# Sampling stream 1.7 images behind the gated stream instead of two, both streams made continuous, and the preparation of the next image moved to steps 89 to 186

## Chip, core and metric

The kernel runs on one core of a Trainium2 chip. The metric is device time in microseconds (us) of one execution; the time before is 12707.76 us, the median of three runs (12704.01 to 12716.35). All engines of the core work from their own in-order instruction streams: PE (TensorE, matmul), DVE (VectorE), ACT (ScalarE), POOL (GpSimd) and SP (SyncE, which here only starts transfers).

## What is computed

The input is 32 images of 128 channels by 32 by 32 pixels. Two layers follow each other, both with a residual:

```python
x = x + L0(_gn(x))      # group norm, encode 128->1024, causal 64-tap convolution per feature, gelu,
                        # gated linear unit 1024->2048, layer norm, decode 1024->128
x = x + L1(_gn(x))      # group norm, depthwise 3x3 conv gives offsets, 8x8 taps sampled bilinearly
                        # at (pixel + tap + offset), weighted per channel, batch norm, gelu
```

Layer 1 shares its offsets over all channels of a tap, so the kernel writes bilinear sampling as a matmul of image rows with hat functions max(0, 1 - |x - i|) times max(0, 1 - |y - j|).

## The kernel before

`ssm_convolution` (L186 on) does the group norm of layer 0, the encoding and the long convolution for all images, and leaves y in DRAM (`y_d`). `main_block` then does the rest in two streams that are woven together by hand; its instruction order is the order of the Python calls (`tc.manual_schedule()`), engine by engine.

**The gated stream** is `first_part(b)`, one image at a time: two halves of 512 pixels, eight feature blocks m each. A block is eight matmuls for the gate (`gpg`, L814), eight for the value (`gpv`, L837), one for the encoding (`gph`, L853) and one decode matmul (`gpo`, L742), all with 512 columns. ACT makes the sigmoid of the gate (`gs`, L821) and a square (`gq`, L874); DVE joins the terms (L845, L866); POOL sums for the layer norm (L738). Three PSUM buffers (`pglu`) rotate through gate, value and encoding. `close` (L764 on) ends a half: two matmuls with `davg` (`gpm`, `gpq`), of which ACT copies the first (`gm`, L765), and some ticks later a store of layer 0's result `x1_d` (L789).

**The sampling stream** is `second_part(b, steps)`: 17 packs of columns. For pack h, SP loads the x hats (`ds<-dhat`, L1116, two buffers) and the y hats (`dhy<-rel_d`, L1131, three half-pack buffers); ACT turns the y distances into hats (`hat_y`, L1151 and L1152); DVE multiplies both (`weights`, L1157); PE multiplies with the image windows (`dps`, L1233) into four PSUM buffers (`psam`); DVE scales by the tap weights (`prod`, L1249); POOL adds up (L1276, L1284). A pack counts as 12 steps, so an image has 204; a full pack has 16 slots, pack 8 has 8, the packs at the ends have 13 or 14.

**The preparation of the next image**, `prepare(b + 1)`, is a list of (step, action) that `second_part(b)` runs in its `due` calls: `fetch` x1 (SP), group norm (`total`, `mean`, `variance`, `normal` on ACT, PE and DVE), nine convolution taps (DVE), two `turn` (PE transposes, ACT copies), 16 `window` transfers, `largest`, `across`, `down` (DVE), two `lay` and four `spread` transfers that lay the distances out in DRAM (`rel_n`, `rel_d`), `gather` (`dr<-rel_d`, L1005), and eight `hat(k)`: ACT computes one of the eight x hats in two instructions (L1016, L1017) into the only buffer of its pool (`hatpool`, 1 buffer) and starts its store on ACT's own queue (`dhat<-dh`, L1018). So hat k waits until the store of hat k-1 has landed. `gather` reads only the x half of `rel_d`, which the first two spreads write. The transfers of SP and ACT take turns at eight completion semaphores, and each waits for the transfer that had its semaphore before, so that about eight are under way at most.

`run_along` (L578 on) weaves generators: it always advances the one whose done share of its total is smallest. Before, `first_part(0)` runs alone, `first_part(1)` runs with `opening()` (the preparation of image 0, then the first loads, given the total 90.0 and yielding 30 plus 51 steps of 1), then `first_part(b + 2)` runs with `second_part(b)`, each pair to its common end, and the last two images are sampled alone.

Of the kernel before, what the change touches and what calls it, by code (L numbers as in the profile page):

```python
# [16 lines left out]
B, C, H, W = 32, 128, 32, 32  # L17
# [559 lines left out]
def run_along(*streams):  # L577


    left = [[gen, float(total), 0.0] for gen, total in streams]  # L580
    while left:
        s = min(left, key=lambda e: e[2] / e[1])
        cost = next(s[0], None)
        if cost is None:
            left.remove(s)
        else:
            s[2] += cost


def main_block(nc, tc, const, ins, x, u_d, y_d, x1_d, out, offmax):  # L590
# [16 lines left out]
    T = 512  # L607
    YB = 11
    SB, HB = 2, 3
    KS = 16 * H  # L610
    ctx = ExitStack()
    with ctx:
# [78 lines left out]
        for i in range(2):  # L691
# [9 lines left out]
        prods = [  # L701
            one.tile([P, 8 * KS + H], F32, tag=f"prod{i}", name=f"prod{i}") for i in range(2)
        ]
# [3 lines left out]
        def at(t, offset, ap):  # L707
            return bass.AP(tensor=t.tensor, offset=t.offset + offset, ap=ap)
# [176 lines left out]
        FIRST = 2 * (KD * (2 * KD + 2) + 2) * MM  # L885
# [4 lines left out]
        def prepare(b):  # L890
# [37 lines left out]
            def taps(lo, hi):  # L928
                def run():
                    if lo == 0:  # L930
                        st["co"] = two.tile([P, L], F32, tag="img", name=f"dco_{b}")
                    co3 = st["co"].rearrange("p (h w) -> p h w", w=W)
                    v3 = st["v"].rearrange("p (h w) -> p h w", w=W)
                    for n in (4, 0, 1, 2, 3, 5, 6, 7, 8)[lo:hi]:
                        dy, dx = n // 3 - 1, n % 3 - 1
                        y0, y1 = max(0, -dy), H - max(0, dy)
                        x0, x1 = max(0, -dx), W - max(0, dx)
                        src = v3[:, y0 + dy : y1 + dy, x0 + dx : x1 + dx]
                        to = co3[:, y0:y1, x0:x1]
                        wn = off_w[:, n : n + 1]  # L940
                        if n == 4:
                            nc.vector.tensor_scalar(
                                to, src, wn, off_b, op0=ALU.mult, op1=ALU.add
                            )
                        else:
                            nc.vector.scalar_tensor_tensor(
                                to, src, wn, to, op0=ALU.mult, op1=ALU.add
                            )

                return run  # L950
# [25 lines left out]
            def lay(a):  # L976
                def run():
                    nc.sync.dma_start(
                        at(
                            rel_n[b % 2], a * ASTEP + LEAST + 7 * JSTEP,  # L980
                            [[KSTEP, 8], [-JSTEP, 8], [1, L]],
                        ),
                        st["rel"][a * 64 : a * 64 + 64].rearrange("p w h -> p (w h)"),
                    )

                return run

            def spread(a, side):
                def run():
                    nc.sync.dma_start(  # L990
                        at(
                            rel_d[b % 2], a * NCOL + side * SIDE,
                            [[NV, 64], [8 * CELLS, NU], [1, NV]],
                        ),
                        at(
                            rel_n[b % 2], a * ASTEP + LEAST - 7 * H + VBASE[side],
                            [[KSTEP - 1, 64], [H, NU], [1, NV]],
                        ),
                    )

                return run
# [7 lines left out]
            def hat(k):  # L1009


                def run():
                    if k == 0:
                        st["h"] = dram.tile([2, 8, SIDE], F32, tag="hat_d", name=f"dhat_{b}")
                    t = hatpool.tile([P, HSUB], F32, tag="hat", name=f"dh_{b}_{k}")
                    nc.scalar.activation(t, st["t"], AF.Abs, bias=minus[:, k : k + 1])  # L1016
                    nc.scalar.activation(t, t, AF.Relu, scale=-1.0, bias=const["one"])  # L1017
                    nc.scalar.dma_start(  # L1018
                        at(
                            st["h"], k * SIDE,  # L1020
                            [[HSUB, P // 2], [8 * SIDE, 2], [1, HSUB]],
                        ),
                        t,
                    )

                return run

            def turn(n):


                def run():
                    if n == 0:
                        st["vt"] = two.tile([P, NCHUNK, C], F32, tag="img", name=f"dvt_{b}")
                    ps = psam.tile([P, 4, C], F32, tag="sam", name=f"dtr_{b}_{n}")
                    for i in range(4):
                        lo = (4 * n + i) * P
                        nc.tensor.transpose(ps[:, i, :], st["v"][:, lo : lo + P], ident)
                    nc.scalar.copy(st["vt"][:, 4 * n : 4 * n + 4, :], ps)
                    if n == 1:
                        st["vt_d"] = dram.tile([L, C], F32, tag="vt_d", name=f"dvt_d_{b}")  # L1040
                        nc.scalar.dma_start(
                            st["vt_d"].rearrange("(n p) c -> p n c", p=P), st["vt"]
                        )
                        st["xw_d"] = dram.tile(
                            [2, W, 8, NWIN, C], F32, tag="xw_d", name=f"dxw_d_{b}"
                        )

                return run

            def window(side, r):  # L1050
                def run():
                    nc.sync.dma_start(
                        st["xw_d"][side, :, r],
                        at(
                            st["vt_d"], (12 * side + r) * W * C,
                            [[C, W], [2 * W * C, NWIN], [1, C]],
                        ),
                    )

                return run  # L1060

            def ready():
                images[b] = st["xw_d"], st["h"]

            steps = [
                (28, fetch), (35, total), (37, mean), (40, variance), (42, normal),
                *((44 + 3 * i, taps(i, i + 1)) for i in range(9)),
                (47, turn(0)), (50, turn(1)),
                *((54 + i, window(i // 8, i % 8)) for i in range(16)),
                (68, largest), (70, across), (74, down), (76, lay(0)), (77, lay(1)),  # L1070
                *((81 + 3 * i, spread(i // 2, i % 2)) for i in range(4)),
                (99, gather), *((109 + 9 * k, hat(k)) for k in range(8)),
                (178, ready),
            ]
            return steps

        NP = len(PACKS)
# [99 lines left out]
        def second_part(b, steps):  # L1177
# [6 lines left out]
            for n in range(NP):  # L1184
# [9 lines left out]
                for i in range(0, PIECES, 2):  # L1194
# [47 lines left out]
                    def scale(piece, side):  # L1242
                        for p, sd, frm, (ky, rows, v0, run, step, skew) in work:
                            if (p, sd) != (piece, side):
                                continue
                            wt = wk[:, table_of[n] : table_of[n] + m]
                            wt = wt[:, :, ky : ky + step * (rows - 1) + 1 : step]
                            at_y = prod[:, ky * KS + v0 - ky :]
                            nc.vector.tensor_mul(  # L1249
# [3 lines left out]
                                        at_y.ap[0], [H, m],  # L1253
                                        [step * (KS - 1) + skew, rows], [1, run],
                                    ],
# [15 lines left out]
                def row(ky, lo=0, hi=m):  # L1271
                    return prod[:, ky * KS + lo * H : ky * KS + hi * H]

# [30 lines left out]
        def measure(slots):  # L1304

            return slots * 8.0 + 40.0

        SECOND = 3 * PIECES * sum(measure(slots_of(n)) for n in range(NP))

        def opening():  # L1310

            yield 30.0
            for _, step in prepare(0):
                step()
                yield 1.0
            for i in range(SB):
                load_x(i)
            for i in range(HB):
                load_y(i)
            windows(0, 0)  # L1320
            for part in range(PARTS):
                hat_y(0, part)
                weights(0, part)
# [1 line left out]

        ctx.enter_context(tc.manual_schedule())
        run_along((first_part(0), FIRST))
        run_along((first_part(1), FIRST), (opening(), 90.0))
        for b in range(B):
            steps = prepare(b + 1) if b + 1 < B else []  # L1330
            if b + 2 < B:
                run_along(
                    (first_part(b + 2, last=(b + 2 == B - 1)), FIRST),
                    (second_part(b, steps), SECOND),
                )
            else:
                run_along((second_part(b, steps), SECOND))
        for _, step in ending:
            step()

# [144 lines left out]
```

## Time and profile before

| | |
|---|---|
| Median of three runs | 12707.76 us |
| The profiled execution | 12713.35 us, of which the span from first to last instruction is 12711.4 us |
| PE busy | 12198.8 us (96%) |
| POOL busy | 8975.3 us (71%) |
| DVE busy | 7803.7 us (61%) |
| ACT busy | 5485.8 us (43%) |
| Sampling, all `dps` matmuls | 23936 matmul instructions, 2753.9 us |
| Gate and value, `gpg` and `gpv` | 16384 matmul instructions, 7499.4 us |
| DMA | 2350.46 MB, 185 GB/s on the mean |
| Granted TensorE clock, mean | 0.973 |

Every float32 matmul shows as two matmul instructions. Busy times come from the profiled execution; a view by stages says more than these shares, because the kernel has stretches with and without each stream. In the stages the granted clock is given as a share of full speed, and DMA share is the mean busy share of the 16 DMA engines.

### The profile page before, as it was taken

How to read it: one execution, taken by the hardware profiler on the slowest of the kernel's cores; microseconds unless marked ns; L12 is line 12 of the kernel's file. 1: busy time of each engine (PE TensorE's matmuls, PEld its weight loads, DVE VectorE, ACT ScalarE, POOL GpSimd, SP SyncE). 2: the span in 40 equal slices, each digit the busy share in tenths (PEclk: the TensorE clock that was granted, in tenths of full speed). 3: DMA queues.
4: the chain of work that ended last, by engine and by line, in shares of the span. 5: the costliest groups of instructions: out<-in, count | busy, mean ns of one | idle time of the engine just before them, and what ended most of it. 6: DMA issues, size and time to landing. Idle time of an engine off the chain costs nothing.

```text
span 12711.4 us, 162031 instructions
## 1 busy us (share of the span) xinstructions
PE 12198.8 (96%) x51362; PEld 6670.1 (52%) x51362; DVE 7803.7 (61%) x14315; ACT 5485.8 (43%) x7823; POOL 8975.3 (71%) x11691
## 2 busy tenths in 40 slices
PE   7999899999999999999999999999999999999965
PEld 7999444444444444444444444444444444444444
DVE  5555126666666666666666666666666666666666
ACT  4344124444444444444444444444444444444443
POOL 2455127777777777777777777777777777777779
PEclk9999999999999999999999999999999999999976
DMA  7899236666766666667666676666666667667666
GB/s 237 266 277 277 74 82 181 180 183 186 188 179 179 177 177 188 181 177 186 179 185 180 185 188 180 178 176 177 188 180 182 184 179 186 181 181 188 180 183 182
DMA packets 1521951, 2350.46 MB, mean 185 GB/s; under 512 B 619586, under 2 KB 835266, under 8 KB 1520066
## 3 DMA queue, kind: packets, MB, share of 16 engines
q1 hardware_dynamic: 1382210, 2027.97, 60.4%
q10 hardware_dynamic: 89728, 177.76, 3.8%
q0 software_dynamic: 49152, 134.28, 3.5%
q8 instruction: 413, 6.77, 0.2%
q14 instruction: 448, 3.67, 0.1%
HBM read 2016.61 MB, written 407.02 MB: 191 GB/s over the span
## 4 chain that ended last, share of the span: by engine, by line
PE 81%; DMA 6%; POOL 5%; DVE 3%; SPq 2%; issue 2%; ACT 1%; ACTq 0%; DVEq 0%; POOLq 0%
PE gpv L837 25%; PE gpg L814 24%; PE dps L1233 16%; PE psy L320 5%; PE gph L853 3%; PE psz L237 3%; DMA ds<-dhat 3%; PE gpo L742 3%; POOL prod L1276 3%; POOL do L1295 1%; DMA dhy<-rel_d 1%; POOL gs L738 1%; SPq L1131 1%; DVE ds L1157 1%; DVE prod L1249 1%
## 5 line engine op out<-in xcount | busy, mean ns | idle before, releaser
L1276 POOL TENSOR_TENSOR prod<-prod 128x256 f32<-128x256 f32 (+3 forms) x7616 | 5797.4, 801 | 1112.8 <-DVE prod L1249 1112.8
L1249 DVE TENSOR_TENSOR prod<-dps,k_weight_slots 128x512 f32<-128x512 f32 (+16 forms) x8704 | 3124.2, 407 | 1615.3 <-PE dps L1233 1204.5
L814 PE MATMUL gpg<-gy,g_w_glu 128*128 128x512 f32 x8192 | 3759.6, 602 | 41.0 <-ACT gs L821 26.9
L837 PE MATMUL gpv<-gy,g_w_glu 128*128 128x512 f32 x8192 | 3739.8, 599 | 0.0
L1233 PE MATMUL dps<-ds,dxw 64*128 64x128 f32 (+14 forms) x23936 | 2753.9, 374 | 262.5 <-DVE prod L1249 229.6
L1157 DVE TENSOR_TENSOR ds<-ds,dhy 128x640 f32<-128x640 f32 (+2 forms) x2176 | 2363.9, 1127 | 784.5 <-ACT dhy L1152 426.9
L1233 PEld LDWEIGHTS dps<-ds,dxw 64*128 64x128 f32 x23936 | 1968.0, 196 | 1343.1 <-issue 432.0
L814 PEld LDWEIGHTS gpg<-gy,g_w_glu 128*128 128x128 f32 x8192 | 1519.9, 191 | 1963.2 <-issue 1907.1
L837 PEld LDWEIGHTS gpv<-gy,g_w_glu 128*128 128x128 f32 x8192 | 1509.7, 190 | 1878.6 <-issue 1878.6
L738 POOL TENSOR_TENSOR gs<-gs,gq 128x256 f32<-128x256 f32 x896 | 751.5, 859 | 1856.7 <-ACT gq L874 1856.7
L1151 ACT ACTIVATE dhy<-dhy,k_minus_y 128x640 f32<-128x640 f32 (+2 forms) x2176 | 1698.5, 781 | 483.4 <-DMA dhy<-rel_d 174.0
L1152 ACT ACTIVATE dhy<-dhy,one 128x640 f32<-128x640 f32 (+2 forms) x2176 | 1726.5, 793 | 71.1
L874 ACT ACTIVATE gq<-gr 128x512 f32<-128x512 f32 x448 | 281.3, 628 | 2557.7 <-DVE gr L866 2551.8
L845 DVE SCALAR_TENSOR_TENSOR gs<-gpv,k_b_glu,gs 128x512 f32<-128x512 f32 x512 | 383.9, 750 | 1357.8 <-PE gpv L837 1289.4
L821 ACT ACTIVATE gs<-gpg,k_b_glu 128x512 f32<-128x512 f32 x512 | 351.3, 686 | 1860.7 <-PE gpg L814 1846.8
L357 POOL DMA_DIRECT2D y_d<-yo x1024 | 590.0, 583 | 693.5 <-ACT yo L344 633.5
L1284 POOL TENSOR_TENSOR dacc<-dacc,prod 128x256 f32<-128x256 f32 (+6 forms) x1184 | 886.7, 749 | 55.2
L738 POOL TENSOR_TENSOR gs<-gs,gr 128x256 f32<-128x256 f32 x896 | 810.7, 925 | 0.0
L320 PE MATMUL psy<-toe,z 128*128 128x192 f32 x4096 | 668.0, 326 | 7.4 <-DVE z L242 5.5
L320 PEld LDWEIGHTS psy<-toe,z 128*128 128x128 f32 x4096 | 663.0, 196 | 11.7 <-DVE z L242 6.8
L335 DVE TENSOR_TENSOR psy<-psy,t 128x256 f32<-128x256 f32 (+2 forms) x768 | 333.7, 434 | 346.1 <-ACT t L328 329.3
L853 PE MATMUL gph<-gu,k_W_enc 128*128 128x512 f32 x1024 | 530.2, 600 | 0.4 <-DVE gs L845 0.4
(164 smaller groups left out, 6055.0 us busy)
## 6 DMA issues: line engine op xcount, KB each, us to landing
dhy<-rel_d SPq DMA_DIRECT2D x3264, 160.0 KB
ds<-dhat SPq DMA_DIRECT2D x832, 400.0 KB
ds<-dhat SPq DMA_DIRECT2D x448, 480.0 KB
dxw<-dxw_d SPq DMA_DIRECT2D x832, 224.0 KB
y_d<-yo POOLq DMA_DIRECT2D x1024, 128.0 KB, 4.2
gy<-y_d SPq DMA_DIRECT2D x512, 256.0 KB
u<-u_d SPq DMA_DIRECT2D x224, 512.0 KB
dhat<-dh ACTq DMA_DIRECT2D x256, 390.0 KB
```

What stands on the lines that cost most here:

```text
L320: nc.tensor.matmul(ps[:, c // 2, c % 2, :], rows[i][:, (g * CG + c0 + c) // 2, c % 2, :], toe[:, c0 + c, :], start=True, stop=True,)
L738: nc.gpsimd.tensor_add(to[:, cut], to[:, cut], more[:, cut])
L814: nc.tensor.matmul(gate, w_glu[:, k, D + m * P : D + m * P + P], ys[k], start=(k == 0), stop=(k == KD - 1),)
L837: nc.tensor.matmul(val, w_glu[:, k, m * P : m * P + P], ys[k], start=(k == 0), stop=(k == KD - 1),)
L853: nc.tensor.matmul(h, w_enc[:, m * P : (m + 1) * P], u, start=True, stop=True)
L1151: nc.scalar.activation(t, t, AF.Abs, bias=minus_y)
L1152: nc.scalar.activation(t, t, AF.Relu, scale=-1.0, bias=const["one"])
L1157: nc.vector.tensor_mul(s_of[h][:, cut], s_of[h][:, cut], t)
L1233: nc.tensor.matmul(to[side][:, :, :, r0:r1], xw[half, w, :], frm, start=True, stop=True,)
L1249: nc.vector.tensor_mul(bass.AP(tensor=at_y.tensor, offset=at_y.offset, ap=[at_y.ap[0], [H, m], [step * (KS - 1) + skew, rows], [1, run],], ...
L1276: nc.gpsimd.tensor_add(row(to, lo, hi), row(to, lo, hi), row(frm, lo, hi))
L1284: nc.gpsimd.tensor_add(to, to, total[:, slot * H : (slot + nj) * H].rearrange("p (s y) -> p s y", y=H),)
```

## The change

The streams become two generators, woven once: all gated images from 1 on, and `opening()` followed by all sampled images. Each image counts 1 in its stream, and `opening()` counts AHEAD = 0.7 in place of a whole image. The preparation steps get new numbers, and are sorted: the distance between hats is 4 steps in place of 9, and `gather` stands at 150, ahead of the last of the spreads (151). In `opening()` the steps are now in sorted order too.

```diff
+    AHEAD = 0.7
...
-                (28, fetch), (35, total), (37, mean), (40, variance), (42, normal),
-                *((44 + 3 * i, taps(i, i + 1)) for i in range(9)),
-                (47, turn(0)), (50, turn(1)),
-                *((54 + i, window(i // 8, i % 8)) for i in range(16)),
-                (68, largest), (70, across), (74, down), (76, lay(0)), (77, lay(1)),
-                *((81 + 3 * i, spread(i // 2, i % 2)) for i in range(4)),
-                (99, gather), *((109 + 9 * k, hat(k)) for k in range(8)),
-                (178, ready),
+                (89, fetch), (94, total), (96, mean), (99, variance), (101, normal),
+                *((103 + 3 * i, taps(i, i + 1)) for i in range(9)),
+                (106, turn(0)), (109, turn(1)),
+                *((113 + i, window(i // 8, i % 8)) for i in range(16)),
+                (129, largest), (131, across), (135, down), (137, lay(0)), (138, lay(1)),
+                *((142 + 3 * i, spread(i // 2, i % 2)) for i in range(4)),
+                (150, gather), *((154 + 4 * k, hat(k)) for k in range(8)),
+                (186, ready),
             ]
+            steps.sort(key=lambda e: e[0])
...
-        run_along((first_part(1), FIRST), (opening(), 90.0))
-        for b in range(B):
-            steps = prepare(b + 1) if b + 1 < B else []
-            if b + 2 < B:
-                run_along(
-                    (first_part(b + 2, last=(b + 2 == B - 1)), FIRST),
-                    (second_part(b, steps), SECOND),
-                )
-            else:
-                run_along((second_part(b, steps), SECOND))
+
+        def first_parts():
+
+            for b in range(1, B):
+                for cost in first_part(b, last=(b == B - 1)):
+                    yield cost / FIRST
+
+        def second_parts():
+
+            for cost in opening():
+                yield AHEAD * cost / 82.0
+            for b in range(B):
+                steps = prepare(b + 1) if b + 1 < B else []
+                for cost in second_part(b, steps):
+                    yield cost / SECOND
+
+        run_along((first_parts(), 1.0), (second_parts(), 1.0))
```

## Prediction

> **What bounds the kernel now.** I read the stages first, because the kernel has stretches with one stream and with both. The columns are stage, length, busy time of PE, PE's weight load, DVE, ACT and POOL, granted clock, DMA share and GB/s.
>
> ```profile
> core 0: us, PE busy (x) PEld busy (x) DVE busy (x) ACT busy (x) POOL busy (x), PEclk, DMA share, GB/s
> 1313.80:1572.70 258.90, 254.84 (x578) 111.39 (x579) 29.25 (x39) 26.22 (x37) 36.00 (x52) 0.97 0.11 39
> 1572.70:1854.90 282.20, 255.35 (x598) 113.10 (x597) 57.51 (x67) 57.29 (x76) 45.82 (x56) 0.95 0.26 68
> 1854.90:2195.40 340.50, 339.53 (x1347) 167.43 (x1345) 216.16 (x404) 151.64 (x204) 242.36 (x314) 1.00 0.66 177
> 12179.00:12449.20 270.20, 143.71 (x761) 111.17 (x760) 186.94 (x360) 130.48 (x170) 217.31 (x272) 0.61 0.77 202
> 12449.20:12680.20 231.00, 137.95 (x747) 109.50 (x748) 170.06 (x338) 97.58 (x126) 213.19 (x270) 0.63 0.72 197
> 12680.20:12711.40 31.20, 0.92 (x4) 0.15 (x3) 3.41 (x10) 1.15 (x1) 19.87 (x28) 0.50 0.06 20
> ```
>
> The rows are: gated image 0 alone; gated image 1 with the opening; one of 30 woven images; image 30 sampled alone, with the preparation of 31; image 31 alone; the rest. The 30 woven images take 12179.0 - 1854.9 = 10324.1 us, 344.1 each, with PE always at work: they are bound by PE. The last two images, 501.2 us, leave PE half idle. A gated image costs 258.9 us alone, so sampling costs 344.1 - 258.9 = 85 us when woven in and 231 us when alone. That difference is what a shorter lag can win. PE's waits in the woven stretch come next:
>
> ```profile
> PE gpm L764 <- POOL gs L738: 61.4, 30, 2.4
> PE dps L1233 <- DVE prod L1249: 43.7, 40, 3.8
> ```
>
> About 2.0 us an image at `gpm`, which the change leaves alone, and 1.5 us at `dps`. So there is next to nothing to win inside a woven image, and whatever newly stops PE is paid 30 times. Where the 1.5 us arises shows in 12 us windows of image 10:
>
> ```profile
> 5422.00:5434.00 12.00, 12.00 (x40) 5.62 (x39) 9.31 (x11) 2.88 (x5) 11.92 (x15) 1.00 0.41 139
> 5434.00:5446.00 12.00, 12.00 (x51) 5.92 (x50) 4.79 (x15) 3.67 (x8) 11.92 (x18) 1.00 0.97 128
> 5458.00:5470.00 12.00, 12.00 (x65) 6.60 (x65) 4.33 (x15) 3.84 (x5) 7.02 (x11) 1.00 1.04 277
> 5470.00:5482.00 12.00, 8.37 (x35) 5.48 (x34) 7.31 (x19) 3.55 (x4) 5.66 (x14) 0.72 0.92 228
> ```
>
> The spreads (issued from 5432 to 5448) fill the DMA engines (0.97, then 1.04); `ds` for the next pack comes late, DVE waits for it, PE loses 3.6 us. `gather`, behind gate inputs and `ds` in the same queue, makes ACT wait 11.56 us before hat 0, which costs nothing there, because ACT runs that far ahead of its place.
>
> **The change, part by part.** The program order of the changed kernel puts the start of gated image b + 2 into pack 5 of sampled image b: the lag is 1.69 images (81/82 of 0.7 for the opening). No computing instruction is added or removed, and POOL and its queue get nothing new to wait for.
>
> *Start.* Gated image 1 now runs 0.69 alone and 0.31 woven: 0.69 x 258.9 + 0.31 x 344.1 = 285.3 instead of 258.9: +26 us.
>
> *Opening.* Its stall is 282.2 - 258.9 = 23.3 us, and looks so:
>
> ```profile
> 1810.85 0.94 ACT L1016 ACTIVATE dh<-dr,k_minus 128x780 f32<-128x780 f32 x1 [1.50 <-DMA dhat<-dh]
> 1828.93 0.69 ACT L1151 ACTIVATE dhy<-dhy,k_minus_y 128x480 f32<-128x480 f32 x1 [16.16 <-DMA dhy<-rel_d]
> 1835.77 0.67 ACT L821 ACTIVATE gs<-gpg,k_b_glu 128x512 f32<-128x512 f32 x1
> 1836.49 9.97 PE L814 MATMUL gpg<-gy,g_w_glu 128*128 128x512 f32 x16 [25.28 <-ACT gs L821]
> ```
>
> ACT is held by the hat stores and the first y hats, the sigmoid queues behind, PE stands. Hats there start every 4.67 us (1806.19 to 1810.85), the opening's step was 258.9/90 = 2.88 us and becomes 0.7 x 258.9/82 = 2.21 us. The hats fall behind by 8 x 0.67 = 5 us more; the 26 us of gated work that followed the opening no longer covers the loads of pack 1, some 5 to 9 us. Bounds 0 and 25; I take +14 us.
>
> *Tail.* The first 5.2 packs of image 30 are now woven. By image 31's pack times (12.2, 18.3, 15.0, 14.5, 14.4, then 0.23 of 14.4, from the `dps` starts), they save 78 us; the preparation, 39 us (270.2 - 231.0), stays in the tail whole, since it begins at step 89. It is squeezed: 32 steps for eight hats are 32 x 1.13 = 36 us at 231/204 us a step, and a hat that had to wait took 7.45 us in this stage:
>
> ```profile
> 12367.83 0.93 ACT L1016 ACTIVATE dh<-dr,k_minus 128x780 f32<-128x780 f32 x1
> 12375.28 0.94 ACT L1016 ACTIVATE dh<-dr,k_minus 128x780 f32<-128x780 f32 x1 [3.19 <-DMA dhat<-dh]
> ```
>
> Eight are 60 us, 24 more than the steps give; bounds 0 and 25, I take +17. Tail: -61 us.
>
> *Woven images.* Fetch, group norm, taps, turns and windows keep their distances, and 0.69 of an image later they meet the gated stream where they met it before; the work, DVE and ACT under 65% busy, hides as before. Variance to normal falls into the short pack 8 (13 us instead of 20.7): ACT's 1.15 us square and 1.28 us table load then stand closer before a PE matmul, 0 to 1 us, I take 0.5. Spreads now fall in packs 11 and 12, followed by full packs, where before pack 8, half as big, gave relief. But `gather` now waits on SP for spread 1, ahead of the five gate loads; `dhy`, the last spread and `ds` of pack 14 queue behind it, and DVE and PE wait for those. Before, three spread issues held SP for 10.4 us anyway, so I see 0 to 4 us more of SP and, since `ds` now precedes the gate loads, about as much back. I let the old 1.6 us (1.5 as above and a trifle at `gpg`) go.
>
> What is new is the hats. Behind hat k on ACT stand `hat_y` of the next packs (DVE and then `dps` wait for them), the sigmoid and the copy `gm`; PE's next gate reuses `gpm`'s buffer and needs `gm` at once: in image 10, `gpm` ran at 5492.3, `gm` at 5493.3, the gate at 5494.9. In the changed order hat 5 stands just ahead of `gm`, with 6.5 us of PE work between (`dps` 2.2, four to five matmuls of 0.86), of which hat and copy need 2.6: ACT may be 4 us late. From hat 0 to hat 5 there are 20 steps of 20.7/12 us = 34.5 us. Five hats of 7.45 us need 37.3; hat 0 itself waits some 2.5 us for `gather` (three spreads ahead of it, 4 steps instead of 10). Late by 37.3 + 2.5 - 34.5 - 4 = 1.3 us. But the 7.45 us was in a stage of DMA share 0.77. The trace's packet records put the end of a hat store 2.3 us after its issue when the engines are idle (all of image 0), 7 to 8 us for hats 0 and 1 of nearly all later images, where the share is 0.9 to 1.0, and 3 to 4.5 us where it is below 0.6. In the new window the demand is: three packs at 11.5 us of all engines, spreads 13, gather 1.4, hats 6.4, gate inputs 4.2, about 60 of 65 us, where the old one measured 0.84. With two stores of 7.7, one of 5.6 and two of 4.4 us, each plus 2.35 us of ACT work and signalling, five hats take 41.6 us: late by 5.6 us. Between 1.3 and 5.6 I take 3.5.
>
> The Trainium skill's page "DMA: Bandwidth & Descriptors" (section "Anatomy of one DMA — SWDGE (gpsimd) path", so for GpSimd's transfers) prices one at a fixed 2.0 us plus bytes over 436 GB/s: 399 KB would land after 2.9 us, a hat would take 4.9 us, inside the 6.9 us of four steps, no wait at all; the woven image would gain 1.6. The opening's 4.67 us agrees with that, the woven images' 7 to 8 us don't. The same page (section "Issuing engines are not separate DMA queues") says why ACT's own queue is no way round: all issuers share 16 engines. I go by the rows of the loaded stretch.
>
> Sum an image: +3.5 + 0.5 - 1.6 = +2.4 us; 30 x 2.4 = +72. Total: 26 + 14 - 61 + 72 = +51 us on 12713.35, that is 12764; the runs' median lies 5.6 us lower, so 12759 us.
>
> **Rivals.** *The hats keep step* (on the other side): if a hat takes at most 7.2 us, (34.5 + 4 - 2.5)/5, ACT is never late and the spread's stall goes. Then the image gains 1.6, 48 us in all, and with the start and tail (-21) the time is 12708 - 69, about 12640. For it: the 4.67 and 7.45 us rows. Against it: the stores of 7 to 8 us. Chance 0.28.
>
> *A wash:* what the hats cost, the spread gives back; only start and tail remain, 12687 us. Chance 0.17.
>
> *Saturation throughout:* a hat takes 9 us to hat 5, late by 45 + 2.5 - 38.5 = 9 us, 7.9 net, 237 - 21 = +216: 12924 us. For it: spreads followed by full packs, `ds` late too. Against it: a stopped PE lets the DMA engines catch up. Chance 0.16. The likeliest case, 12733 to 12830, has 0.39.
>
> That the change does not do what it says is ruled out by the program order.
>
> **Range and chances.** About 0.2% (25 us) is what a measurement of this kernel can tell from no change. Faster 0.28, within 0.17, slower 0.55. From 12625 (a third of the first rival is below) to 12910 (half of the last is above): the cost of a woven image from -2 to +7.5 us.
>
> **What would show it.** A PE wait at `gpg` for ACT (`gm`) or at `dps` for DVE in packs 14 and 15 of every image, with ACT's `dh` waiting for `dhat<-dh` some 5 times an image (9 in all before): right. Woven images under 343 us: the first rival. Opening stall near 37 us and a tail of 470 us after the last gate confirm start and tail. If PE's new wait is for `gy` or `ds`, I priced the queue wrongly.

## The result, and the profile after

The changed kernel takes 12572.62 us (median of four runs, 12565.29 to 12590.62), beside 12709.51 us for the kernel before on the same chip: a ratio of 0.9893, 95% interval 0.988 to 0.9907. It is faster by 1.1%, where 0.4% slower was forecast. The profiled execution was the slowest of the four, 12590.62 us, its span 12588.9 us; so the profiles differ by 122.5 us and the medians by 136.9.

These are stages with the same columns as in the prediction. The first row is the kernel before, over its woven images from gated image 2 to 30. The others are the changed kernel: the same 29 images, one of them, the last woven image (31), image 30 alone, image 31 alone, the rest.

```profile
1854.90:11828.90 9974.00, 9870.93 (x38977) 4879.78 (x38976) 6403.01 (x11687) 4467.69 (x5972) 7571.55 (x9638) 0.99 0.68 181
1898.70:11777.20 9878.50, 9802.21 (x38978) 4834.91 (x38977) 6270.75 (x11688) 4522.82 (x6003) 7410.23 (x9658) 1.00 0.68 183
4968.40:5310.60 342.20, 337.90 (x1345) 166.47 (x1344) 215.48 (x404) 156.12 (x207) 254.94 (x334) 1.00 0.68 182
11777.20:12122.00 344.80, 339.45 (x1347) 167.02 (x1345) 217.18 (x411) 156.63 (x208) 258.30 (x337) 1.00 0.66 177
12122.00:12326.60 204.60, 105.05 (x516) 76.94 (x516) 132.56 (x248) 93.31 (x124) 140.52 (x175) 0.59 0.74 190
12326.60:12556.80 230.20, 138.29 (x747) 108.01 (x748) 169.51 (x338) 98.19 (x126) 214.65 (x271) 0.63 0.73 199
12556.80:12588.90 32.10, 0.85 (x4) 0.11 (x2) 3.36 (x10) 1.15 (x1) 19.83 (x28) 0.50 0.05 19
```

The time moved as follows. The last woven image ends in this table with its last gated matmul, at 12179.0 us before and 12126.5 us after; the rows above cut it 4.5 us sooner, at 12122.0.

| stretch, us | before | after | difference | predicted |
|---|---|---|---|---|
| start, to gated image 2 | 1854.9 | 1898.7 | +43.8 | +40 |
| 29 woven images, gated 2 to 30 | 9974.0 | 9878.5 | -95.5 | with the 30th: |
| woven image with gated 31 | 350.1 | 349.3 | -0.8 | +72 |
| after the last gate | 532.4 | 462.4 | -70.0 | -61 |
| span | 12711.4 | 12588.9 | -122.5 | +51 |

Start and end came within 9 us of the forecast. Nearly the whole error lies inside the woven images: 343.93 us each before, 340.64 after. Over the 29 images PE is busy for 9870.93 us before and 9802.21 us after, with the same matmuls. So PE not only waits less, its matmuls themselves take 68.7 us less. PE's waits in the woven stretch after are (total us, times, longest):

```profile
PE dtr L1038 <- DVE prod L1251: 34.1, 29, 1.2
PE gph L854 <- DVE gs L846: 26.2, 24, 3.1
PE dps L1235 <- DVE prod L1251: 12.0, 17, 1.1
PE gpm L765 <- POOL gs L739: 2.5, 3, 1.0
```

The wait at `gpm`, which the prediction left alone, is gone (61.4 us, 30 times, before), and so is most of that at `dps`. Two new ones, at `dtr` and `gph`, come once an image each but are short: of all waits over half a microsecond in these images, eight are longer than 1.3 us.

**Why `gpm` waits no more.** In the kernel before, this is POOL's timeline at the end of an image (start, duration, operation, count, idle time before):

```profile
5294.42 10.52 POOL L1276 TENSOR_TENSOR prod<-prod 128x224 f32<-128x224 f32 x14
5304.91 1.91 POOL L1284 TENSOR_TENSOR dacc<-dacc,prod 128x160 f32<-128x160 f32 x4
5306.92 4.69 POOL L1295 TENSOR_SCALAR do<-dacc,k_bn_mean,k_bn_var 128x1024 f32<-128x1024 f32 x1
5311.67 0.95 POOL L1183 MEMSET dacc<- 128x1024 f32 x1
5312.59 2.39 POOL L738 TENSOR_TENSOR gs<-gs,gr 128x256 f32<-128x256 f32 x2
```

and this PE at the same place:

```profile
5310.72 2.29 PE L1233 MATMUL dps<-ds,dxw 64*128 64x156 f32 x28
5315.03 1.13 PE L764 MATMUL gpm<-gs,davg 128*128 128x512 f32 x2 [2.02 <-POOL gs L738]
```

The sums `gs` that `gpm` reads stand in POOL's queue behind the last samples and the scaling of the finished image. Both streams were cut at the same place, so the end of a gated image always met the end of a sampled image. After the change, POOL where the second half of a gated image closes reads:

```profile
4972.74 2.58 POOL L739 TENSOR_TENSOR gs<-gs,gr 128x256 f32<-128x256 f32 x2
4979.07 9.62 POOL L1278 TENSOR_TENSOR prod<-prod 128x256 f32<-128x256 f32 x14 [3.75 <-DVE prod L1251]
```

and PE:

```profile
4986.35 1.98 PE L838 MATMUL gpv<-gy,g_w_glu 128*128 128x512 f32 x4
4988.18 1.02 PE L765 MATMUL gpm<-gs,davg 128*128 128x512 f32 x2
```

The sum is done at 4975.3, 13 us before `gpm` wants it, and POOL even idles 3.75 us in between.

**What a wait costs.** The granted clock tells the other half. In the kernel before, a stall of 3.63 us ends at 5474.73 us; 28 `dps` matmuls of the form 64x192 follow. Their line, and the window over just these matmuls, are

```profile
5474.73 4.95 PE L1233 MATMUL dps<-ds,dxw 64*128 64x192 f32 x28 [3.63 <-DVE prod L1249]
5474.73:5479.68 4.95, 4.95 (x29) 4.17 (x29) 3.32 (x14) 1.89 (x2) 3.34 (x9) 0.50 0.81 205
```

PE is busy all through, at half its clock. After the change, 28 matmuls of the same form took 2.55 us where PE came to them without a stall:

```profile
4983.87 2.55 PE L1235 MATMUL dps<-ds,dxw 64*128 64x192 f32 x28
```

Half clock covers 130 us of the 29 woven images before (29 records of 3.4 or 6.8 us in the trace), which costs about half of that, 65 us. Of the 130 us, 65 follow a wait at `gpm` (18 of its 28 waits have a record behind them) and 65 a wait at `dps`. After, half clock covers 7 us in two records. So 61.5 of the 68.7 us that PE's busy time lost are half clock that went; the other 7 are not explained.

An image's arithmetic is as follows. A wait is counted here, and in the experiments, from start to start of PE's matmuls, less their usual distance, and only above half a microsecond, so that each is about 0.15 us longer than in the rows of waits. Waits: 3.92 us before and 2.87 after, -1.05. Half of the half clock: 2.24 and 0.12, -2.12. The rest: 337.77 and 337.65. Together that is -3.29 us, as the stages say. The rows alone give the same sum without this way of counting: PE's idle time fell from 103.1 to 76.3 us, -0.92 an image, and its busy time by 2.37 an image.

### The profile page after: what moved, and what is told of

Same layout as the page of the kernel before. It is cut to its first block, busy times and chain, and to the rows that moved or that the text cites. A ratio compares the mean times of both kernels' runs of the same rounds, so it can differ in the third digit from the quotient of the medians.

```text
span 12588.9 us, 161534 instructions
## 1 busy us (share of the span) xinstructions
PE 12115.7 (96%) x51362; PEld 6608.0 (52%) x51362; DVE 7661.0 (61%) x14315; ACT 5537.8 (44%) x7852; POOL 8789.7 (70%) x11691
## 3 DMA queue, kind: packets, MB, share of 16 engines
q14 instruction: 443, 3.63, 0.1%
## 4 chain that ended last, share of the span: by engine, by line
PE 77%; DMA 10%; ACT 5%; DVE 3%; issue 2%; SPq 2%; POOL 1%; ACTq 0%; DVEq 0%; POOLq 0%
PE gpv L838 24%; PE gpg L815 23%; PE dps L1235 15%; DMA dhat<-dh 5%; PE psy L320 5%; PE psz L237 3%; PE gpo L743 3%; PE gph L854 3%; DMA rel_d<-rel_n 1%; ACT dh L1018 1%; ACT dh L1017 1%; ACT dhy L1153 1%; POOL prod L1278 1%; DVE ds L1159 1%; DMA dr<-rel_d 1%
## 5 line engine op out<-in xcount | busy, mean ns | idle before, releaser
L1278 POOL TENSOR_TENSOR prod<-prod 128x256 f32<-128x256 f32 (+3 forms) x7616 | 5531.4, 767 | 1211.5 <-DVE prod L1251 1211.5
L1235 PE MATMUL dps<-ds,dxw 64*128 64x128 f32 (+14 forms) x23936 | 2700.2, 371 | 235.4 <-DVE prod L1251 171.5
L1159 DVE TENSOR_TENSOR ds<-ds,dhy 128x640 f32<-128x640 f32 (+2 forms) x2176 | 2260.0, 1075 | 929.0 <-ACT dhy L1154 673.3
L1235 PEld LDWEIGHTS dps<-ds,dxw 64*128 64x128 f32 x23936 | 1924.2, 194 | 1287.3 <-issue 480.6
L739 POOL TENSOR_TENSOR gs<-gs,gq 128x256 f32<-128x256 f32 x896 | 865.7, 987 | 1820.8 <-ACT gq L875 1820.8
```

What stands on the lines that cost most here:

```text
L739: nc.gpsimd.tensor_add(to[:, cut], to[:, cut], more[:, cut])
L1159: nc.vector.tensor_mul(s_of[h][:, cut], s_of[h][:, cut], t)
L1235: nc.tensor.matmul(to[side][:, :, :, r0:r1], xw[half, w, :], frm, start=True, stop=True,)
L1278: nc.gpsimd.tensor_add(row(to, lo, hi), row(to, lo, hi), row(frm, lo, hi))
```

## Experiments

The theory tested, P: the gain is in PE's waits and in the half clock behind them; `gpm` lost its wait because of the *phase*, the place of the gated stream's ends against POOL's queue. Rivals: S, the new step numbers bring it (spreads into full packs, `gather` early, other hats); K, that both streams are continuous. In the results below, "waits" are PE's per woven image, longer than half a microsecond, and "half" is the half clock in 29 images, in us. The batches ran on different chips (the kernel before took 12709 to 12846 us on them), so each ratio is against the kernel before on its own chip. The image times, waits and half clock come from one profile each and are not corrected for the chip; on the slowest one the kernel before ran at a mean granted clock of 0.967 where it had 0.973 above, and some 4 us an image of a profile there can be the chip's.

**New steps at the old lag.** The kernel after, with

```diff
-    AHEAD = 0.7
+    AHEAD = 82.0 / 81.0
```

> The changed kernel with the opening counted as a whole image (AHEAD = 82/81), so that both streams end their images together again, with the new preparation steps kept. Theory P (the ends of the two images no longer fall together: POOL's end-of-image work held up gpm, and PE's clock was halved after it): woven images back at 343 to 345 us, gpm waiting for POOL about 2 us an image, time 12690 to 12730. Theory S (the new places of spread, gather and hats did it): woven images stay at 340 to 341.5, time 12600 to 12640, since start and tail go back to those of before.

Measured: 12934.2 us, ratio 1.0146 (1.0128 to 1.0164). A woven image takes 351.11 us. Half is 208 us, and the waits are 6.49 us: `gpm` still 2.04, `dtr` 2.32, `dps` in pack 15 1.17.

```profile
PE dtr L1038 <- DVE prod L1251: 60.2, 28, 2.8
PE dps L1235 <- DVE prod L1251: 56.8, 119, 1.8
PE gpm L765 <- POOL gs L739: 55.0, 27, 2.1
```

The steps alone cost 1.5%, so S is false as a whole. P had the sign but not the size: of the 7.2 us that an image is longer than before, the waits and the half clock account for 3.9, and the rest is not explained. The wait one pack behind the spreads (pack 8 before, it would be 13 here) isn't among the larger ones, which is the part of S that stands.

**Old steps, continuous streams.** The same woven loop with AHEAD at 82/81 and the steps of the kernel before.

> The continuous streams alone: AHEAD = 82/81 and the old preparation steps. P and S both: as before, 12695 to 12725, woven images 343 to 345 us. Theory K (the common end of each pair of streams in the old weave cost something by itself): below 12680.

It took 12749.01 us, ratio 1.0002 (0.9993 to 1.0011), with waits of 2.15 us at `gpm` and 2.1 us at `dps` an image, half 174 us. K is false.

**Old steps, lag 2.3.** As before, with AHEAD at 1.3.

> Old preparation steps with a longer lag: AHEAD = 1.3, so the sampled image ends 0.28 of an image after the gated one. Start and tail together cost about 0.28 x (231 - 85) = 41 us more than at a lag of 2. P: the gpm wait of 2 us an image goes, woven images 340.5 to 342.5, so 30 x 2.5 = 75 us less, time 12660 to 12695. S: woven images 344, time 12740 to 12760.

It took 12774.1 us, ratio 1.0021 (1.0013 to 1.0029), with 344.98 us an image: P's forecast failed, and S's came true. Here the ends of the streams lie apart, and `gpm` waits 2.75 us all the same, now in pack 4:

```profile
PE gpm L765 <- POOL gs L739: 75.0, 29, 2.6
```

In POOL's timeline of one such place, 14 products and two sums of an ordinary pack (13.87 and 1.52 us) stand just ahead of the `gs` that `gpm` waits for. So the common end is not the only thing that makes the wait; what counts is what stands in POOL's queue at that moment.

**The end-of-image scaling taken off POOL.** The kernel before, with the scaling done in ACT's gelu and `dacc` cleared at step 8:

```diff
-            nc.gpsimd.tensor_scalar(
-                o.rearrange("p (h w) -> p w h", w=W), acc, bn_mean, bn_inv,
-                op0=ALU.subtract, op1=ALU.mult,
-            )
-            ending.append((6, lambda: nc.scalar.activation(o, o, AF.Gelu, bias=bn_beta)))
+            ending.append((6, lambda: nc.scalar.activation(
+                o.rearrange("p (h w) -> p w h", w=W), acc, AF.Gelu,
+                bias=bn_shift, scale=bn_inv,
+            )))
```

> The kernel before, with POOL's end-of-image scaling (4.7 us an image) folded into ACT's gelu as its scale and bias, and the clearing of the sum moved to step 8; lag and preparation steps as before. The result is the same up to rounding. P: the gpm wait falls from 2.0 us to under 0.5 an image and the half-clock stretches after it go: woven images 340.5 to 342.5, time 12610 to 12660. S: gpm's wait may go, but only its own 57 us at most without a clock share; below that only 5 us at the very end: 12650 to 12705.

It took 12690.95 us, ratio 0.9956 (0.994 to 0.9973). Its waits of PE are

```profile
PE dps L1240 <- DVE prod L1256: 82.1, 57, 5.4
PE gph L856 <- DVE gs L848: 1.2, 3, 0.5
```

`gpm` is not in the list any more, so at this phase it was POOL's 4.69 us operation, with the clearing behind it, that made it wait. But `dps` has 82.1 us where it had 43.7, and half clock stayed at 133 us, now all of it behind `dps`. So P was right on `gpm` and wrong on the rest: the image takes 343.36 us, where it expected 342.5 at most.

**The same in the kernel after.**

> The changed kernel with POOL's end-of-image scaling folded into ACT's gelu and the clearing at step 8, as was done to the kernel before. There it took away the gpm wait; here gpm does not wait (2.5 us in all), so P expects little: 0 to 20 us less (POOL's 4.7 us at the very end, ratio 0.9875 to 0.989). If POOL's load by itself were the cause of the slow woven images, another 30 us or more should go (ratio below 0.987).

It took 12605.2 us, ratio 0.991 (0.9893 to 0.9926): no gain over the kernel after, where the operation hides already.

**The wait put back.** The kernel after, with one more operation of POOL ahead of `gpm`:

```diff
+            nc.gpsimd.tensor_scalar(sums[0], sums[0], 1.0, None, op0=ALU.mult)
```

> The changed kernel with one more POOL instruction ahead of each gpm (the layer norm's sum times 1.0, about 1.5 to 2 us), so that gpm has to wait for POOL behind the pack sums; nothing else is changed. Theory P (a PE stall costs its length and a half-clock stretch after it): where the wait is about 2 us or more, half-clock stretches of 3.4 to 6.8 us come back, and woven images grow by more than the waits themselves, by about 1.5 to 2 times their sum. Rival (the clock has another cause): images grow by just the waits. For 2 to 4 us of waits an image: 60 to 120 us in all by the rival, 100 to 220 by P.

It took 12739.32 us, ratio 1.0015 (1.0008 to 1.0022); the whole gain is gone. An image takes 345.94 us, 5.3 more. The waits grew by 3.66 us, and half clock from 7 to 123 us, worth 2.0 us an image; 109 us of it follow the waits at `gpm` that were put in, most of them where the first half of an image closes. A microsecond of waiting here costs some 1.5, as P expected, and this is the most direct evidence for the second half of the arithmetic above.

**The hats closer.**

```diff
-                (150, gather), *((154 + 4 * k, hat(k)) for k in range(8)),
+                (150, gather), *((154 + 2 * k, hat(k)) for k in range(8)),
```

> The changed kernel with the hats 2 steps apart instead of 4 (154 to 168). By the step of the prediction that priced the hats (what ACT is late by, less 4 us, stops PE), five hats then need some 36 us in a window of 17 us, ACT is over 15 us late, and every image loses 10 us or more: +300 us on the changed kernel, ratio to before 1.013 or more. Theory Q (ACT's lateness is mostly hidden, since what waits for it has slack of its own): +0 to +60 us, ratio 0.99 to 0.994.

It took 13196.15 us, ratio 1.0374 (1.0357 to 1.0392), with 360.73 us an image.

```profile
PE gpm L765 <- POOL gs L739: 223.4, 27, 9.9
PE dps L1235 <- DVE prod L1251: 196.4, 27, 8.5
```

Nothing but the distance of the hats was changed, so hats that come too close do stop PE: at `dps`, as the prediction reasoned, and at `gpm`, which it did not name. An image loses 20 us, twice the 10 that were expected as the least; 652 us of half clock are part of it.

**The hats wider.** The kernel after with hats at 152 + 5k and `ready` at 188.

> The changed kernel with hats 5 steps apart (152 to 187, ready 188). If the waits at gph in pack 14 and dps in pack 15 (1.0 and 0.3 us an image) are the hats' doing, they go: 20 to 40 us less than the changed kernel, ratio to before 0.986 to 0.9885. If they have another cause: 0.989 to 0.991.

It took 12553.07 us, ratio 0.9846 (0.983 to 0.9863): faster than the kernel after (0.9893) by more than expected, and its image of 339.53 us is the shortest of all. The waits:

```profile
PE dtr L1038 <- DVE prod L1251: 34.4, 29, 1.4
PE gpm L765 <- POOL gs L739: 13.4, 21, 1.3
PE gph L854 <- DVE gs L846: 2.3, 4, 0.7
```

`gph` has 2.3 us where it had 26.2, and `dps` is off the list: these two, 1.3 us an image, were what the hats cost at 4 steps. `gpm` took 0.4 us of it back. No record of half clock is left.

**`gather` two steps later.** The kernel after with `gather` at 152, two steps ahead of hat 0.

> The changed kernel with gather at step 152, after the last spread. The hats start later by the spread's time (some 5 us) while their steps stay: as the hats stand at the edge of what ACT can be late by, P expects 2 to 6 us an image more, ratio to before 0.995 to 1.005. If gather's place is of no weight here: 0.989 to 0.991.

It took 12775.44 us, ratio 1.0017 (1.0009 to 1.0026): the place of `gather` alone is worth more than the whole gain. Hat 0 in ACT's timeline of one image, and PE a little later:

```profile
5527.57 0.94 ACT L1017 ACTIVATE dh<-dr,k_minus 128x780 f32<-128x780 f32 x1 [9.87 <-DMA dr<-rel_d]
5528.55 0.95 ACT L1018 ACTIVATE dh<-dh,one 128x780 f32<-128x780 f32 x1
5529.53 0.55 ACTq L1019 DMA_DIRECT2D dhat<-dh  x1
5530.18 0.83 ACT L1153 ACTIVATE dhy<-dhy,k_minus_y 128x640 f32<-128x640 f32 x1 [0.69 <-ACT dh L1018]
```

```profile
5546.38 1.00 PE L1235 MATMUL dps<-ds,dxw 64*128 64x192 f32 x2 [4.72 <-DVE prod L1251]
```

ACT stands 9.87 us for `gather` and 5.04 us more for the store of hat 0. The next y hats (`dhy`) stand behind that, DVE waits 9.01 us for them, and PE then waits 4.72 us for DVE. In the kernel after, hat 0 waits 0.64 us.

**`gather` early in the kernel before** (89 for 99).

> The kernel before with one number changed: gather at step 89 instead of 99, so ahead of the last spread and of the gate inputs, as in the changed kernel; lag 2 and all else as before. P: the PE wait at dps in pack 8 (1.6 us an image before) falls below 0.5 and its half-clock stretches go, gpm's 2 us stay: images 341.5 to 343, time 30 to 70 us less, ratio 0.9945 to 0.9976. If the gather's place has no part in it (the spreads themselves or the packs they meet do): ratio 0.999 to 1.001.

It took 12817.92 us, ratio 1.0056 (1.004 to 1.0073), slower where a gain was expected: a miss. ACT's wait for `gather` (254.6 us before) is no longer among its ten largest, but `dps` lost 3.49 us an image in pack 8 instead of 1.61. ACT's wait had cost nothing there; that the earlier transfer delays the loads behind it is likely, but only argued.

**The turns later.** The kernel after with the turns at 109 and 112 and the windows from 116.

> The changed kernel with the two turns and the windows three steps later (turn 109 and 112, windows from 116), so that PE's transposes no longer come before DVE has made the normalised image in the short pack 8. The wait of 1.3 us an image at dtr should go: P expects 25 to 45 us less than the changed kernel (ratio to before 0.9855 to 0.9875). If the stall only moves to a later matmul: as the changed kernel, 0.989.

It took 12599.35 us, ratio 0.9906 (0.9889 to 0.9922). The `dtr` wait went, the one at `gph` grew to 1.5 us, and the image takes 341.18 us: moved, not won.

**Another phase.** The kernel after with AHEAD = 0.85.

> The changed kernel with the opening counted 0.85: a lag of 1.84. Start and tail cost about 0.15 x (231 - 85) = 22 us more than at 1.69, the opening has 39 us more room for its stall of 43 us and gives perhaps 10 back. Everything else is the phase between the two streams: at 1.69 images take 340.6, at 2 with the same steps 351. If the phase matters smoothly, 343 to 347 us an image and a ratio to before near 1.0; if only the common end of the two images at 2 is bad, 340 to 341.5 us and a ratio of 0.990 to 0.9915.

It took 12839.88 us, ratio 1.0076 (1.0059 to 1.0092), with 348.66 us an image: worse than either forecast. There is no wait at `gpm`, but 7.09 us of others (`dtr` 2.57, `dps` 1.95 and 1.44 in two packs); half is 259 us.

**The wide hats at AHEAD = 0.75.**

> The version with the wide hats (152 + 5k, ready at 188), with 0.75 for 0.7 as the lead of the sampled stream, so that the gated stream stands 0.05 image (some 17 us) elsewhere against all steps. Theory P (the waits of PE depend on where the gated stream's short operations fall against the queues of POOL, DVE and ACT, in units of one pack or less): stalls of PE of 4 us or more an image come back in at least one place, 0.990 to 1.005 of the kernel before, against 0.985 with 0.7. Rival S (any lag near 1.7 does it, what counts is that the ends of the two streams lie apart): 0.983 to 0.987.

It took 12779.99 us, ratio 0.9949 (0.9935 to 0.9963), as P expected: two thirds of the gain of the wide hats are lost by moving one stream some 17 us.

```profile
PE gpg L815 <- DMA gy<-y_d: 199.7, 56, 6.8
```

Again another wait: now the gate's own inputs stand in SP's queue between the spreads. A lag near 1.7 alone does not do it.

**The spreads later in the kernel before.**

```diff
-                *((81 + 3 * i, spread(i // 2, i % 2)) for i in range(4)),
-                (99, gather), *((109 + 9 * k, hat(k)) for k in range(8)),
-                (178, ready),
+                *((105 + 3 * i, spread(i // 2, i % 2)) for i in range(4)),
+                (123, gather), *((131 + 7 * k, hat(k)) for k in range(8)),
+                (188, ready),
```

> The kernel before, with the four spreads at steps 105 to 114 (end of the short pack 8, and pack 9) where they stood at 81 to 90, gather at 123, hats at 131 + 7k, ready at 188; nothing else is changed. Theory P (the spread's stall at dps comes from the short pack 8, whose samples need their loads twice as soon after the spreads): the 1.6 us an image at dps in pack 8 and most of the half clock behind it go, the wait at gpm (2.1 us) stays, 0.992 to 0.996 of the kernel before. Rival S (the stall follows the spreads wherever they stand, since they fill the DMA engines): it turns up again about two packs behind them, with 1.5 us or more an image, 0.999 to 1.01.

It took 12795.69 us, ratio 0.9962 (0.9949 to 0.9976). The wait in pack 8 goes, some 0.8 us at `dps` in packs 10 and 11 come, and `gph` in pack 9 waits 2.27 us for DVE, whose `ds` waited 556.8 us in all for its loads (225.0 before) over the stretch. The ratio lies at the edge of P's range, and the trace has something of both: the short pack made the spread's wait at `dps`, but DVE still waits for late loads, and PE for DVE elsewhere. The waits and the half clock (5.18 us, 150 us) are no fewer than before in a profile of another chip, so where this gain comes from is open.

**The wide hats with POOL's scaling gone.**

> The version with the wide hats, with POOL's scaling at the end of an image folded into ACT's gelu and the clearing of acc moved to step 8. Theory P (what is left at gpm, 0.5 us an image in pack 14, comes from POOL's weights of the samples, not from the end of the image): no gain in the woven images, only the tail ends some 5 us sooner, 0.984 to 0.9855. Rival S (POOL's load as a whole makes the wait): the 0.5 us go too, 0.981 to 0.983.

It took 12630.7 us, ratio 0.9831 (0.9817 to 0.9844), on a chip where the kernel before takes 12846 us; its interval overlaps that of the wide hats. `gpm` still waits 0.7 us, so its remaining wait isn't that operation. PE also waits 47.1 us in all for the gate inputs `gy`, which it did not with the wide hats on the other chip; why is open.

## Why the prediction was wrong

**Start, opening, tail: right.** The opening's stall was put near 37 us and measured 43.0:

```profile
1790.96 4.13 PE L1235 MATMUL dps<-ds,dxw 64*128 64x168 f32 x28 [43.02 <-DVE ds L1159]
```

After the last gate 470 us were forecast, 462.4 came.

**The failed step: "About 2.0 us an image at `gpm`, which the change leaves alone" and "next to nothing to win inside a woven image".** The wait was read, and even its releaser was in the row (`POOL gs`), but what stood ahead of `gs` on POOL wasn't looked at. It was a queue of the *other* stream, and the change shifts the two streams by 0.3 of an image against each other: such a wait can go by the shift alone. (It went at lags of 1.69 and 1.84 and stayed at 2 and 2.3.) It measured -2.0 us an image (2.12 to 0.10). By the sign named for the first rival, images under 343 us, the result is on that rival's side, but its reason holds in part only: the hats were not free, and the larger part of the gain, `gpm` and the clock, it left at nothing too. They carried the time a further 67 us below its 12640. Nothing in the forecast looked at the phase, so that the new one is a good one was luck.

**The term that was missing: the half clock.** The 0.72 in the window with the 3.6 us stall was shown in the prediction and not priced. It is worth 2.1 us an image, half of it behind `gpm` and half behind `dps`. This is the count over all 17 traced kernels, of waits of PE in 29 woven images as the rows show them, and of those with half clock begun between their start and 8 us after their end:

| wait, us | number | with half clock |
|---|---|---|
| 0.5 to 1 | 204 | 37 |
| 1 to 1.5 | 292 | 21 |
| 1.5 to 2.5 | 357 | 225 |
| 2.5 to 4 | 155 | 128 |
| over 4 | 105 | 102 |

Of the 482 records of half clock in these stretches, 478 begin there. They last 3.4 us or a small multiple of it (3.4 in 263, 6.8 in 131). The Trainium skill's page "TensorE: Matmul & The Clock Gate" (section "🔬 Part 1: The HAM clock gate (the "warmup" mystery)") says that the gate halves the clock after an idle window of about 3.4 us. The lengths agree with that window. By that sentence alone, the 2.0 us waits at `gpm` would cost no clock, and the lost term would have been small. The traces say otherwise for waits that short, and the measurement decides. So the change did not only shorten the waits: it replaced waits of 2 to 4 us by pieces of about 1.2, which mostly keep the clock.

**The hats: mechanism right, size wrong.** The sign on ACT came as named, five waits an image. PE pays 1.3 us of it, not 3.5, at `gph` in pack 14 and `dps` in pack 15, and not at `gpg`. These are ACT's waits in all, and hats 0 to 5 of one image in its timeline:

```profile
ACT dh L1017 <- DMA dhat<-dh: 317.3, 145, 4.4
...
5120.79 0.94 ACT L1017 ACTIVATE dh<-dr,k_minus 128x780 f32<-128x780 f32 x1 [0.64 <-DMA dr<-rel_d]
...
5132.26 0.94 ACT L1017 ACTIVATE dh<-dr,k_minus 128x780 f32<-128x780 f32 x1 [3.62 <-DMA dhat<-dh]
...
5141.82 0.95 ACT L1017 ACTIVATE dh<-dr,k_minus 128x780 f32<-128x780 f32 x1 [2.14 <-DMA dhat<-dh]
...
5148.62 0.94 ACT L1017 ACTIVATE dh<-dr,k_minus 128x780 f32<-128x780 f32 x1 [3.64 <-DMA dhat<-dh]
...
5154.10 0.95 ACT L1017 ACTIVATE dh<-dr,k_minus 128x780 f32<-128x780 f32 x1 [0.90 <-DMA dhat<-dh]
...
5160.85 0.93 ACT L1017 ACTIVATE dh<-dr,k_minus 128x780 f32<-128x780 f32 x1
```

Hat 5 waits for nothing any more. By the medians of all images the first five stores took 7.5, 6.9, 4.1, 3.4 and 2.3 us from issue to landing, 24.2 in all, where 29.8 was assumed; with 2.35 us of ACT each that is 36 us instead of 41.6. From hat 0 to hat 5, with all that ACT did between, 38.7 us went by (median; 36.8 to 40.1), and the 2.5 us for `gather` shrank to 0.64 in the image shown, since it stood early enough. That makes ACT late by about 38.7 + 0.6 - 34.5 - 4 = 0.8 us in the prediction's sum, where it had 1.3 to 5.6 and took 3.5. The medians fall from hat to hat: the loaded rows of the prediction had been carried on to stores that came after the load. (One of its readings was off as well: in the kernel before, the stores of hat 0 took 6.5 us on the median, not 7 to 8; those of hat 1 took 8.0.)

**The spread's wait, -1.6 us: right** (1.61 and 0.18 at `gpg` before, none there after). With the new steps it is gone at lag 2 also. Part of the lateness of the loads may still turn up elsewhere, as with the moved spreads.

**Short pack 8, +0.5 us: too small, and for another cause.** The turns' transposes (`dtr`) wait there 1.34 us for a PSUM buffer that DVE's `prod` frees. They do so at lag 2, too (2.32 us), and moving them gained nothing.

So the terms of an image, forecast and measured, are: hats +3.5 and +1.3; pack 8 +0.5 and +1.3; spreads -1.6 and -1.8; `gpm` 0 and -2.0; half clock 0 and -2.1. The first sum is +2.4, the second -3.3. The half clock belongs to the waits: counted with it, `gpm` is -3.1 and the spreads are -2.9.

What stays open: the old steps at lag 1.7 have no run, since image b + 1 isn't gated yet when they would start. Phase and steps thus cannot be separated completely. The new steps at lags of 2 and 1.84 lose time, the old ones at 2.3 gain none, and `gpm` follows the phase. Which phases are good was seen at five points only (1.69, 1.74, 1.84, 2, 2.3) and is told by no simple rule. Also, the sum "waits plus half of the half clock plus a constant" does not hold everywhere. With the waits of the rows, the constant is 337.5 to 338.5 us for twelve of the 17 kernels and 339.0 and 339.6 for two; it misses for three, with 342.2 (the new steps at the old lag), 335.2 (the wide hats at AHEAD = 0.75) and 332.9 (the close hats).

## What to carry to other kernels

When a change shifts two woven streams against each other, list every wait of the bounding engine whose releaser belongs to the other stream, and look at what stands ahead of the releaser in its queue: those waits go, or come, by the shift. Price a wait of TensorE of 1.5 us or more with the half-clock time behind it, and ask whether a wait can be cut into pieces of about a microsecond. Where an in-order engine carries work for two streams (here ACT with hats behind a transfer), a few steps of distance decide, and it pays to try them: `gather` by two steps was worth 1.3%, the hats by one step each 0.5%.

## What was not expected of the hardware

- PE waits of 1.5 to 2.5 us in an otherwise full stream came with half clock in 225 of 357 cases, those of 0.5 to 1.5 us in 58 of 496.
- A store of the same 390 KB took 7.5 us from issue to landing beside the spreads and 2.3 us some 33 us later in the same image (hats 0 and 4, medians).
- Half clock shows as PE's busy time, not as waiting: with the same matmuls PE was busy 68.7 us less when 123 us of half clock had gone.
